# Gate logits of a graph network: narrow matrix products on TensorE, or row sums on VectorE in the later superblocks

## Chip, core and metric

The kernel runs on one core of a Trainium2 chip. The metric is device time in microseconds (us) of one execution, given as the median of several runs. A separate execution was taken with the hardware profiler; the lines shown in this document come from its page and its trace.

## What is computed

The reference is a graph network with 10000 nodes of 512 features and 160000 edges, in two layers. What matters here is the first layer, and of it one line:

```
gates = softmax(x @ gate_W + gate_b)          # gate_W is 512 x 4
top_v, top_i = top_k(gates, 2)                # two of four experts for each node
each expert: h = relu(mean_of_neighbours(h) @ Wl + bl + h @ Wr), twice
out = sum over the two chosen experts of top_v * expert output
```

The four numbers `x @ gate_W + gate_b` of a node are its gate logits. The second layer is an attention over the same edges, in which source and destination change their roles, so the edges have to be put in another order for it. The kernel does that sorting itself, during the first layer.

## The kernel before

**Tiling.** The nodes are cut into 79 blocks of 128, one node on each partition. Two blocks are a superblock (the first one has a single block), so there are 40 superblocks, numbered `s` = 0 to 39. The kernel runs in three stages. The first (the loop in lines 1227 to 1282) does the first convolution of all four experts, the gate logits, and the sorting. The second gathers the results for the second convolution and makes queries, keys and values. The third is the attention and what follows it. The change lies in the first stage.

**One superblock of the first stage**, in the order of the code: `drive(more, 1)` runs two of the ten gathering rounds of the next superblock; then come the gate logits of this one; then for each expert `e` the function `conv` (64 products for each `h`, line 1190, with a ScalarE activation into `h`, line 1192), two more gathering rounds, and from `e` = 1 on `products` of the expert before (line 1200, results stored to `y_tab` and `h_tab` in lines 1205 and 1206). At the end `turned_all` transposes the next superblock's rows into `tt` (line 1174), and the last `products` follows.

**Gathering.** A round takes the feature rows of four groups of edges out of a ring of ten buffers, multiplies them with one-hot matrices into `p_ag` (line 1151), and then issues with `pull` (line 1126) the indirect DMAs on GpSimd that fill the buffers used ten places later. `prepare` builds the one-hot matrices for a later block on VectorE (lines 902 and 1137). `load_x` brings the block's own 128 x 512 rows, `xb`, from two buffers; `turned_all` reads them.

**Gate logits.** For each block four products of the transposed rows in `tt` with the 128 x 4 pieces of `gw` go into a PSUM tile `pg` (line 1244), and VectorE adds `gb` to it on the way to `gate_w` (line 1246). In the trace each float32 product is two matrix instructions, so a block has eight and a superblock sixteen. At `s` = 12, 25, 38 and 39 the function `gates` turns the collected logits into the choice of experts.

**Sorting.** The generator `plan_src` counts, on VectorE, how many edges belong to each window of 32 nodes (158 counting steps, line 930) and then searches a slot for each edge. `side`, called after each quarter of a `conv`, advances it. When the search has ended, `side` puts a 1 into the list `planned`, and from then on it advances `scatter_src` instead: groups of 16 indirect DMAs (line 1060) from a tile `pay`, seven DMAs in each `conv`. The first of these starts at 1563.8 us in the trace, between the gate products of superblock 15 (which start at 1552.0 us) and those of superblock 16.

**Order.** In the first stage the order of the instructions on TensorE, VectorE, ScalarE and GpSimd is the order of the code (`manual_schedule`). The queue of SyncE, which issues the plain DMAs, is ordered by the compiler's scheduler. Each engine takes its instructions in that order and waits on semaphores. A pool tile with a `bufs` count is handed out again only after every reader of its former content is done.

Of the kernel before, what the change touches and what calls it, by code (L numbers as in the profile page):

```python
# [8 lines left out]
F32 = mybir.dt.float32  # L9
BF16 = mybir.dt.bfloat16  # L10
# [3 lines left out]
ALU = mybir.AluOpType  # L14
# [4 lines left out]
P = 128  # L19
D = 512  # L20
KD = D // P
NE = 4
# [595 lines left out]
WP = 2 + H  # L618
# [18 lines left out]
def fast(ctx: ExitStack, tc: tile.TileContext, a: dict, out: bass.AP, bad: bass.AP):  # L637
# [8 lines left out]
    nc = tc.nc  # L646
# [3 lines left out]
    NB = -(-N // P)  # L650
    NP = NB * P
    C = E // P
    NW = NB * NQ
# [7 lines left out]
    NPR = NW // 2  # L661
# [36 lines left out]
    def load_w(pool, name, ap, k, n, eng=None):  # L698
        return load_to(pool.tile([P, k, n], F32, name=name), ap, eng)
# [61 lines left out]
    gate_w = mp.tile([P, NB, NE], F32, name="gate_w")  # L761
# [20 lines left out]
    wp = p1.enter_context(tc.tile_pool(name="p1w", bufs=1))  # L782
# [28 lines left out]
    with tc.tile_pool(name="win", bufs=1) as one, tc.tile_pool(name="win2", bufs=2) as two, \  # L811
# [26 lines left out]
        for t in range(T):  # L838
# [8 lines left out]
                                    accum_out=more[:, t:t + 1])  # L847
            b = beg[:, t:t + 1]
            nc.vector.scalar_tensor_tensor(b, row[:, t:t + 1], float(C), more[:, t:t + 1],
                                           op0=ALU.mult, op1=ALU.add)  # L850
# [4 lines left out]
            for dst, flat in ((d_w, flat_d), (s_w, flat_s)):  # L855
# [8 lines left out]
                                           op0=ALU.is_gt, op1=ALU.add)  # L864
# [3 lines left out]
                                           op0=ALU.mult, op1=ALU.add)  # L868
            for c in range(CAP):
                for src, to in ((loc, loc_t[t]), (idx, idx_t[t])):  # L870
# [9 lines left out]
                                op0=ALU.not_equal)  # L880


    for e in range(NE):
        load_to(wl[e], a["L0_gnn_Wl"][e, 0])
        load_to(wr[e], a["L0_gnn_Wr"][e, 0], nc.scalar)
    gw = load_w(wp, "gw", a["L0_gnn_gate_W"], KD, NE)
    gb = wp.tile([P, NE], F32, name="gb")
    nc.sync.dma_start(gb, rows_bcast(a["L0_gnn_gate_b"], NE))
    bl = wp.tile([P, NE, KD], F32, name="bl")
# [18 lines left out]
    SC = max(C, 2 * D)  # L908
# [7 lines left out]
    def plan_src(pool, ps):  # L916
# [3 lines left out]
        pair = pool.tile([P, SC], BF16, name="pair")[:, :C]  # L920
# [7 lines left out]
        for b in range(NPR):  # L928
            m = pool.tile([P, C], BF16, name="m")
            v.scalar_tensor_tensor(m, pair, float(b), digit, op0=ALU.is_equal, op1=ALU.mult,  # L930
                                   accum_out=count[:, b:b + 1])
            yield
        num = pool.tile([P, NPR, 2], F32, name="num")
        even, odd = num[:, :, 0], num[:, :, 1]
        whole(v, odd, count, 1.0 / DIG, -0.4552)
        v.scalar_tensor_tensor(even, odd, -DIG, count, op0=ALU.mult, op1=ALU.add)
        upper = pool.tile([P, P], F32, name="upper")
        nc.gpsimd.iota(upper, pattern=[[1, P]], base=0, channel_multiplier=-1,
                       allow_small_or_imprecise_dtypes=True)
        v.tensor_scalar(upper, upper, 0.0, None, op0=ALU.is_gt)  # L940
        flat = num.rearrange("p b q -> p (b q)")
        total = ps.tile([P, 512], F32, name="mm")
        nc.tensor.matmul(total[:, :NW], ones, flat, start=True, stop=True)
        first = ps.tile([P, 512], F32, name="mm")
# [6 lines left out]
        v.tensor_reduce(top[:, 1:2], total[:, :NW], axis=AX.X, op=ALU.add)  # L951
        v.tensor_scalar(fail[:, 2:3], top[:, 1:2], float(E), None, op0=ALU.not_equal)
        v.tensor_scalar(flat, total[:, :NW], float(SC_W * P), 0.0, op0=ALU.subtract, op1=ALU.max)
        left = pool.tile([P, NB, 2], F32, name="left")
        half = left.rearrange("p b h -> p (b h)")
        v.tensor_add(half, even, odd)
        whole(v, left[:, :, 0], left[:, :, 0], 0.25, 0.375)
        v.scalar_tensor_tensor(left[:, :, 1], left[:, :, 0], 4.0, left[:, :, 1],
                               op0=ALU.mult, op1=ALU.add)
# [80 lines left out]
    GS = 16  # L1040

    def scatter_src(pool):
        src_r = a["src"].rearrange("(p c) -> p c", c=C)
        dst_r = a["dst"].rearrange("(p c) -> p c", c=C)
        att_r = a["edge_attr_8"].rearrange("(p c) h -> p c h", c=C)
        for c0 in range(0, C, GS):
            n = min(GS, C - c0)
            ends = pool.tile([P, 2, GS], I32, name="ends", bufs=2)
            nc.sync.dma_start(ends[:, 0, :n], src_r[:, c0:c0 + n])
            nc.sync.dma_start(ends[:, 1, :n], dst_r[:, c0:c0 + n])  # L1050
            att = pool.tile([P, GS, H], F32, name="att", bufs=2)
            nc.sync.dma_start(att[:, :n, :], att_r[:, c0:c0 + n, :])
            nc.vector.tensor_single_scalar(ends[:, 0, :n], ends[:, 0, :n], P - 1,
                                           op=ALU.bitwise_and)
            pay = pool.tile([P, GS, WP], F32, name="pay", bufs=3)
            nc.gpsimd.tensor_copy(pay.bitcast(I32)[:, :n, 0], ends[:, 1, :n])
            nc.gpsimd.tensor_copy(pay[:, :n, 1], ends[:, 0, :n])
            nc.gpsimd.tensor_copy(pay[:, :n, 2:], att[:, :n, :])
            for c in range(n):
                inst = nc.gpsimd.indirect_dma_start(  # L1060
                    out=sorted1[:],
                    out_offset=bass.IndirectOffsetOnAxis(ap=addr_i[:, c0 + c:c0 + c + 1], axis=0),
                    in_=pay[:, c, :], in_offset=None, bounds_check=P * NC - 1, oob_is_err=False)
                tc.declare_no_dep(inst.ins, group="sorted1", reason="rows of their own")
                tc.add_to_no_dep_group("sorted1", inst.ins)
                yield
# [47 lines left out]
    with p1, tc.tile_pool(name="p1k", bufs=1) as kp, tc.tile_pool(name="p1", bufs=2) as dp, \  # L1114
# [67 lines left out]
            return tt  # L1182

        def conv(tt, e, n):
            h = dp.tile([P, KD, 2 * P], F32, name="h", bufs=4)
            for f in range(KD):
                ph = pm.tile([P, D], F32, name="mm")
                for i, w in enumerate((wl[e], wr[e])):
                    for k in range(KD):
                        nc.tensor.matmul(ph[:, :n], w[:, k, f * P:(f + 1) * P], tt[:, i, k, :n],  # L1190
                                         start=(i + k == 0), stop=(i == 1 and k == KD - 1))
                nc.scalar.activation(h[:, f, :n], ph[:, :n], AF.Relu, bias=bl[:, e, f:f + 1])  # L1192
                side(e, f)
            return h
# [16 lines left out]
        planned, planning = [], [0]  # L1211
# [15 lines left out]
        with tc.manual_schedule(engines={ET.PE, ET.DVE, ET.Activation, ET.Pool}):  # L1227
            for i in range(GB):
                pull(i)
            prepare(0)  # L1230
            gated, GSTEP = 0, 13
            rows = []
            drive(gather(0, rows), CAP)
            tt = turned_all(rows)
            for s in range(NSB):
                n = P * len(rows)
                ahead = []
                more = gather(s + 1, ahead) if s + 1 < NSB else iter(())

                drive(more, 1)  # L1240
                for i, (b, xb, ag) in enumerate(rows):
                    pg = psm.tile([P, NE], F32, name="small")
                    for k in range(KD):
                        nc.tensor.matmul(pg, tt[:, 1, k, i * P:(i + 1) * P], gw[:, k, :],
                                         start=(k == 0), stop=(k == KD - 1))
                    nc.vector.tensor_add(gate_w[:, b, :], pg, gb)
                h = []
                for e in range(NE):
                    h.append(conv(tt, e, n))
                    if s == NSB - 1:  # L1250

                        load_to(wl[e], a["L0_gnn_Wr"][e, 1])
                        if e < 3:
                            nc.scalar.dma_start(wr[e], wqkv_s[e])
                    drive(more, 1)
                    if e == 0:

                        upto = SB[s][-1] + 1
                        if s == NSB - 1 or s % GSTEP == GSTEP - 1:
                            with tc.tile_pool(name="gates", bufs=1) as gt:  # L1260
                                gates(gt, gated, upto)
                            gated = upto
                    else:
                        products(s, h[e - 1], e - 1, n)
                rows = ahead
                if ahead:
                    tt = turned_all(ahead)
                products(s, h[3], 3, n)
                if s >= 1:
                    drive(fill, 11)  # L1270
                if s == max(NSB - 3, 0):
                    drive(plan, 10 ** 6)
                    drive(fill, 10 ** 6)
                    t3 = kp.tile([P, SC], F32, name="scan")[:3]
                    t1 = kp.tile([P, SC], BF16, name="pair")[:3]
                    for i, n in enumerate("qkv"):
                        nc.sync.dma_start(t3[:1, :D], a[f"L1_gnn_b{n}"][None, :])
                        nc.sync.dma_start(t3[:1, D:2 * D], fold_s[i:i + 1, :])
                        nc.vector.tensor_add(t3[:1, :D], t3[:1, :D], t3[:1, D:2 * D])
                        nc.sync.dma_start(bias_s[i:i + 1, :], t3[:1, :D])  # L1280
                    for i, n in enumerate(("bo", "b2")):
                        split_rows(t3[:, :D], t3[:, D:2 * D], t1[:, :D], i, a[f"L1_gnn_{n}"])


    with ExitStack() as p2:
        wp = p2.enter_context(tc.tile_pool(name="p2w", bufs=1))
# [8 lines left out]
        dp = p2.enter_context(tc.tile_pool(name="p2", bufs=2))  # L1295
# [72 lines left out]
        with tc.manual_schedule(engines={ET.PE, ET.Pool}):  # L1368
# [47 lines left out]
            for b in range(NB):  # L1416
                xb = load_x(dp, b)
# [29 lines left out]
                for v in range(2):  # L1447
                    nc.vector.scalar_tensor_tensor(t[v], p_ag[v], inv_deg[:, b:b + 1], t[v],
                                                   op0=ALU.mult, op1=ALU.add)
# [11 lines left out]
    with ExitStack() as p3:  # L1461
        wp = p3.enter_context(tc.tile_pool(name="p3w", bufs=1))
# [487 lines left out]
```

## Time and profile before

| | |
|---|---|
| median of 3 runs | 10796.1 us (10785.83 to 10797.64) |
| the profiled execution, its own time | 10026.75 us |
| span of the profiled execution, first to last instruction | 10025.0 us |
| mean granted TensorE clock in it | 0.981 |
| busy time of TensorE (matrix products) | 9375.0 us, 94% |
| busy time of VectorE | 5435.3 us, 54% |
| busy time of GpSimd | 6933.2 us, 69% |
| gate products (line 1244) | 632 instructions, from 100.5 to 3884.1 us |

The profiled execution is shorter than the runs that were timed. All durations below come from the profiled one. Busy time of an engine is a sum over the span and says nothing about which engine sets the time in a given stretch; for that one looks at a stretch of its own, and at which engine never waits there.

### The profile page before, as it was taken

How to read it: one execution, taken by the hardware profiler on the slowest of the kernel's cores; microseconds unless marked ns; L12 is line 12 of the kernel's file. 1: busy time of each engine (PE TensorE's matmuls, PEld its weight loads, DVE VectorE, ACT ScalarE, POOL GpSimd, SP SyncE). 2: the span in 40 equal slices, each digit the busy share in tenths (PEclk: the TensorE clock that was granted, in tenths of full speed). 3: DMA queues.
4: the chain of work that ended last, by engine and by line, in shares of the span. 5: the costliest groups of instructions: out<-in, count | busy, mean ns of one | idle time of the engine just before them, and what ended most of it. 6: DMA issues, size and time to landing. Idle time of an engine off the chain costs nothing.

```text
span 10025.0 us, 168607 instructions
## 1 busy us (share of the span) xinstructions
PE 9375.0 (94%) x63334; PEld 5488.9 (55%) x63334; DVE 5435.3 (54%) x8330; ACT 2927.5 (29%) x6026; POOL 6933.2 (69%) x6736
## 2 busy tenths in 40 slices
PE   7999999999999999999999999998888888888888
PEld 4666666666666666333333333333555555555555
DVE  7898991000100002445555555555888878888885
ACT  1111111111111111111111111111566666666665
POOL 5566666777777774777777777775666666666664
PEclk9999999999999999999999999998999999999999
DMA  6544455555555554888888888886878877777774
GB/s 213 179 154 155 158 162 162 155 159 156 163 168 156 164 157 160 281 297 298 299 294 300 297 303 302 297 299 215 255 254 257 256 252 252 254 256 255 252 253 132
DMA packets 1077231, 2263.27 MB, mean 226 GB/s; under 512 B 250526, under 2 KB 500260, under 8 KB 1075638
## 3 DMA queue, kind: packets, MB, share of 16 engines
q0 software_dynamic: 588224, 1659.68, 51.6%
q1 hardware_dynamic: 479456, 577.23, 16.6%
q10 hardware_dynamic: 8726, 15.49, 0.4%
q8 instruction: 503, 8.24, 0.3%
q14 instruction: 322, 2.64, 0.1%
HBM read 2181.26 MB, written 379.27 MB: 255 GB/s over the span
## 4 chain that ended last, share of the span: by engine, by line
PE 55%; DMA 16%; issue 9%; DVE 8%; ACT 7%; POOL 5%; POOLq 0%; ACTq 0%; DVEq 0%; SPq 0%
PE mm L1190 21%; PE mm L1200 10%; DMA kv<-kv_all,meta 7%; PE mm L1385 5%; DMA y<-y_tab,ix 5%; PE p_ag L1151 3%; DMA ring<-y_tab,ix 3%; PE p_ag L1426 3%; PE bank L1646 2%; DVE s L1879 2%; DVE m L930 2%; PE bank L1636 2%; PE mm L1347 2%; POOL y L1330 2%; ACT L1638 1%
## 5 line engine op out<-in xcount | busy, mean ns | idle before, releaser
L1126 POOL DMA_INDIRECT ring<-in_x_dram,idx_t x1580 | 1897.1, 1201 | 1014.3 <-PE p_ag L1151 570.3
L1190 PE MATMUL mm<-tt,big 128*128 128x256 f32 (+1 forms) x8960 | 1964.7, 378 | 0.0
L1190 PEld LDWEIGHTS mm<-tt,big 128*128 128x128 f32 x8960 | 1684.3, 191 | 285.3 <-issue 71.2
L1060 POOL DMA_INDIRECT sorted<-pay,addr x1250 | 1280.0, 1024 | 380.4 <-issue 336.8
L1552 POOL DMA_INDIRECT kv<-kv_all,meta x948 | 972.3, 1026 | 260.1 <-issue 144.5
L1330 POOL DMA_INDIRECT y<-y_tab,ix x920 | 947.5, 1030 | 287.8 <-issue 216.9
L1200 PE MATMUL mm<-wn,h 128*128 128x512 f32 x2528 | 1124.0, 598 | 0.0
L1385 PE MATMUL mm<-big,hb 128*128 128x512 f32 x2528 | 1120.4, 597 | 1.7 <-DMA hb<-h_tab 1.7
L1192 ACT ACTIVATE h<-mm,bl 128x256 f32<-128x256 f32 (+1 forms) x640 | 301.2, 471 | 2125.5 <-PE mm L1190 2125.5
L1714 POOL TENSOR_TENSOR ohp<-oh,p 128x768 f32<-128x768 bf16 x316 | 465.8, 1474 | 572.3 <-ACT p L1705 571.0
L1330 POOL DMA_INDIRECT ring<-y_tab,ix x660 | 684.7, 1037 | 228.6 <-issue 150.7
L1347 PE MATMUL mm<-big,z_t 128*128 128x512 f32 x1896 | 829.6, 594 | 0.7 <-ACT z_t L1340 0.7
L1385 PEld LDWEIGHTS mm<-big,hb 128*128 128x128 f32 x2528 | 469.7, 191 | 597.3 <-issue 532.8
L1388 DVE TENSOR_TENSOR mine<-mm,bias 128x512 f32<-128x512 f32 x316 | 218.5, 692 | 1065.2 <-PE mm L1385 1063.6
L1200 PEld LDWEIGHTS mm<-wn,h 128*128 128x128 f32 x2528 | 469.6, 191 | 594.0 <-issue 593.9
L1636 PE MATMUL bank<-big,big 128*128 128x256 f32 (+1 forms) x2560 | 671.7, 410 | 89.6 <-ACT big L1638 89.5
L1843 DVE TENSOR_TENSOR kv<-qe,kv 128x1024 f32<-128x1024 f32 x474 | 576.4, 1216 | 256.2 <-DMA kv<-kv_all,meta 255.1
L1426 PE MATMUL p_ag<-y,oh 128*32 128x512 f32 x3680 | 580.3, 600 | 77.4 <-DMA y<-y_tab,ix 77.1
L902 DVE TENSOR_TENSOR oh<-loc_t,iota_w 128x640 f32<-128x640 bf16 x158 | 131.3, 831 | 928.0 <-PE p_ag L1151 850.1
L1636 PEld LDWEIGHTS bank<-big,big 128*128 128x128 f32 x2560 | 501.2, 204 | 207.9 <-ACT big L1638 113.4
L1347 PEld LDWEIGHTS mm<-big,z_t 128*128 128x128 f32 x1896 | 362.0, 191 | 455.2 <-issue 429.8
L1646 PE MATMUL bank<-big,big 128*128 128x512 f32 x1264 | 592.4, 598 | 1.2 <-ACT big L1620 0.7
(298 smaller groups left out, 13882.7 us busy)
## 6 DMA issues: line engine op xcount, KB each, us to landing
y_tab<-y SPq DMA_DIRECT2D x632, 256.0 KB
hb<-h_tab SPq DMA_DIRECT2D x316, 256.0 KB
h_tab<-h SPq DMA_DIRECT2D x156, 512.0 KB
kv_all<-kvt SPq DMA_DIRECT2D x79, 520.0 KB
xb<-in_x_dram SPq DMA_DIRECT2D x156, 256.0 KB
q_all<-q SPq DMA_DIRECT2D x79, 384.0 KB
q<-q_all SPq DMA_DIRECT2D x237, 128.0 KB
ring<-in_x_dram,idx_t POOLq DMA_INDIRECT x1580
```

Source lines behind the costliest of these rows:

```text
L1060: inst = nc.gpsimd.indirect_dma_start(out=sorted1[:], out_offset=bass.IndirectOffsetOnAxis(ap=addr_i[:, c0 + c:c0 + c + 1], axis=0), in_=p ...
L1126: nc.gpsimd.indirect_dma_start(out=gbuf[i % GB], out_offset=None, in_=x, in_offset=bass.IndirectOffsetOnAxis(ap=window(idx_t, b)[:, j, c:c ...
L1190: nc.tensor.matmul(ph[:, :n], w[:, k, f * P:(f + 1) * P], tt[:, i, k, :n], start=(i + k == 0), stop=(i == 1 and k == KD - 1))
L1200: nc.tensor.matmul(py, h[:, k, i * P:(i + 1) * P], wn[e][:, k, :], start=(k == 0), stop=(k == KD - 1))
L1330: nc.gpsimd.indirect_dma_start(out=ybuf[i % YB], out_offset=None, in_=y_flat, in_offset=bass.IndirectOffsetOnAxis(ap=ahead[b][1][:, j, c:c ...
L1347: nc.tensor.matmul(po, z_t[:, k, :], wqkv[i][:, k, :], start=(k == 0), stop=(k == KD - 1))
L1385: nc.tensor.matmul(pr, hb[:, k, :], wr[e][:, k, :], start=(k == 0), stop=(k == KD - 1))
L1426: nc.tensor.matmul(p_ag[v][j * W:(j + 1) * W, :], oh[:, j * CAP + c, :], g[:, v * D:(v + 1) * D], start=(c == 0), stop=(c == CAP - 1))
L1552: nc.gpsimd.indirect_dma_start(out=to, out_offset=None, in_=kv_all[:], in_offset=bass.IndirectOffsetOnAxis(ap=blocks[b][0].bitcast(I32)[:, ...
L1636: nc.tensor.matmul(ph, up(f, k), z_t[:, k, :m], start=(k == 0), stop=(k == KD - 1))
L1646: nc.tensor.matmul(po, hid[:, k, i * P:(i + 1) * P], w2[k // KD][:, k % KD, :], start=(k == 0), stop=False)
L1843: nc.vector.tensor_tensor(k, qe.pop((w, g)).rearrange("p c (h d) -> p c h d", h=H), k, op=ALU.mult)
```

## The change

For each superblock that comes after the end of the slot search (`planned` is not empty), the gate logits are no longer made by TensorE. VectorE multiplies `xb` with a copy of `gate_W` that lies whole on every partition (`gate_rows`, 512 x 4 values), one column of the four at a time, and sums along the row in the same instruction (`accum_out`); the product itself goes to a tile that nobody reads. Then it adds `gb`. The superblocks ahead of the end of the search keep the products on TensorE.

One more DMA on SyncE's queue loads `gate_rows`. To make room for it, `h` gets three buffers and not four, `pay` gets two and not three, and `num`, `upper` and `left` of the search lie together in a tile that shares its place with the search's other scratch tile `scan`.

```
+    gate_rows = wp.tile([P, D, NE], F32, name="gate_rows")
+    gate_wt = a["L0_gnn_gate_W"]
+    nc.sync.dma_start(gate_rows, bass.AP(tensor=gate_wt.tensor, offset=gate_wt.offset,
+                                         ap=[[0, P], [1, D * NE]]))
     gb = wp.tile([P, NE], F32, name="gb")
...
-        num = pool.tile([P, NPR, 2], F32, name="num")
+        room = pool.tile([P, SC], F32, name="scan")
+        num = room[:, P:P + NW].rearrange("p (b q) -> p b q", q=2)
...
-        upper = pool.tile([P, P], F32, name="upper")
+        upper = room[:, :P]
         nc.gpsimd.iota(upper, pattern=[[1, P]], base=0, channel_multiplier=-1,
...
-        flat = num.rearrange("p b q -> p (b q)")
+        flat = room[:, P:P + NW]
...
-        left = pool.tile([P, NB, 2], F32, name="left")
-        half = left.rearrange("p b h -> p (b h)")
+        left = room[:, P + NW:P + NW + NPR].rearrange("p (b h) -> p b h", h=2)
+        half = room[:, P + NW:P + NW + NPR]
...
-            pay = pool.tile([P, GS, WP], F32, name="pay", bufs=3)
+            pay = pool.tile([P, GS, WP], F32, name="pay", bufs=2)
...
-            h = dp.tile([P, KD, 2 * P], F32, name="h", bufs=4)
+            h = dp.tile([P, KD, 2 * P], F32, name="h", bufs=3)
...
                 for i, (b, xb, ag) in enumerate(rows):
+                    if planned:
+
+                        unread = kp.tile([P, SC], BF16, name="pair")[:, :D]
+                        for e in range(NE):
+                            nc.vector.scalar_tensor_tensor(
+                                unread, xb, 1.0, gate_rows[:, :, e], op0=ALU.mult, op1=ALU.mult,
+                                accum_out=gate_w[:, b, e:e + 1])
+                        nc.vector.tensor_add(gate_w[:, b, :], gate_w[:, b, :], gb)
+                        continue
                     pg = psm.tile([P, NE], F32, name="small")
                     for k in range(KD):
                         nc.tensor.matmul(pg, tt[:, 1, k, i * P:(i + 1) * P], gw[:, k, :],
```

## Prediction, made before the changed kernel had run

> **What bounds the kernel now.** I read the slices first, saw that TensorE is full for most of the first stage, and then asked for busy time by stretches and for the waits of one quiet stretch. The stretches (length, busy time and instruction count of each engine, granted clock, DMA share, GB/s), one with the search of slots on VectorE and one behind it:
>
> ```profile
> 500.00:1000.00 500.00, 500.00 (x2248) 344.77 (x2244) 445.87 (x270) 79.38 (x153) 330.46 (x208) 1.00 0.49 155
> 2000.00:2500.00 500.00, 500.00 (x2236) 343.01 (x2235) 27.19 (x59) 80.07 (x154) 357.72 (x378) 1.00 0.51 159
> ```
>
> TensorE (first pair) has no idle time in either; VectorE (third) falls from 446 us to 27 us; GpSimd (fifth) is at 358. The waits between 2000 and 3500 us (total, times, longest) say who waits for whom:
>
> ```profile
> ACT h L1192 <- PE mm L1190: 813.1, 244, 6.7
> DVE oh L902 <- PE p_ag L1151: 577.6, 31, 22.4
> POOL ring L1126 <- PE p_ag L1151: 121.2, 28, 7.3
> PEld p_ag L1151 <- DMA ring<-in_x_dram,idx_t: 5.0, 15, 0.3
> ```
>
> Everybody waits for TensorE; it waits 0.3 us at most for a gathered row. So this stage lasts as long as TensorE's list of instructions. The chain of waits over one superblock (start, length, what) shows that list without a hole:
>
> ```profile
> 2036.13 1.85 PE p_ag L1151 x16
> 2037.98 1.88 PE small L1244 x16
> 2039.86 13.92 PE mm L1190 x64
> 2053.78 1.00 PE p_ag L1151 x8
> 2054.78 0.31 PE small L1159 x2
> 2055.09 0.99 PE p_ag L1151 x8
> 2056.08 14.01 PE mm L1190 x64
> 2070.09 1.85 PE p_ag L1151 x16
> ```
>
> The gate products (L1244) start again at 2135.17, so a superblock takes 97.19 us, and the gate is 1.88 us of it. The view of that line from 1564 us on counts what the change removes:
>
> ```profile
> L1244 PE MATMUL small<-gw,tt x384: 170/253/274, 1649.2 to 3884.1; 128*128 128x4 f32 x192
>   DVE gate_w L1246: 423.8, 48
> ```
>
> 384 instructions are 24 superblocks of 16, numbers 16 to 39; VectorE waited for them 48 times, once for each block.
>
> [...] 1.88 us over 16 is 118 ns each for 4 columns[...]. [...] The trace has 748 ns for such an instruction, and I use that. [...] pulls (L1126) have a median of 1327 ns from 600 to 1500 us, with VectorE busy, and 998 ns from 2000 to 3500 us. [...]
>
> **The change, part by part.**
>
> 1. *Gate products removed.* 24 superblocks. What follows the products changes its neighbour: conv's 64 products take 13.92 us behind the gate and 14.01 us where they follow p_ag directly (the row at 2056.08). So 1.88 + 13.92 - 14.01 = 1.79 us each, 24 x 1.79 = **43.0 us** off TensorE, all of it on the path. tt has been written by then: the transposes lie a whole set of products (6.87 us) ahead.
>
> 2. *Row sums on VectorE.* Eight for a superblock. Nearest row: the float32 scalar_tensor_tensor of L1394, and for the accumulator's read the 83 ns behind each L930:
>
> ```profile
> L1394 DVE SCALAR_TENSOR_TENSOR t<-mine,pick,t 128x512 f32<-128x512 f32 x474 | 335.1, 748 | 5.5
> L1137 DVE TENSOR_REDUCE slots<-oh 128x128 f32<-128x640 f32 x79 | 99.3, 1257 | 2.7
> L1320 DVE TENSOR_REDUCE at<-mp 128x20 f32<-128x640 f32 x79 | 64.2, 812 | 0.0
> ```
>
> The two reductions read equally many elements, L1137 with a wide step and L1320 in a row: a step can cost 1257/812 = 1.55. So one row sum is 0.83 us at the low end and 748 x 1.55 = 1.16, with the read 1.24 us, at the high end; eight with the two additions are 7.0 to 10.2 us. Cost on the path: **0**. They need only xb, loaded the superblock before, and follow one_hot and slots on VectorE, which end at 2119.9. So they end at 2126.9 to 2130.1. VectorE's next instruction, inv_deg, waits for the L1159 products at 2152: 22 us of cover remain. If VectorE were busy with the search, as up to 1500 us, there would be no such cover; the change leaves those superblocks alone.
>
> 3. *xb is held longer.* Its load for the next superblock now waits for the row sums too. SyncE issues both loads at 2126.28, right behind the transposes:
>
> ```profile
> 2126.28 1.42 SPq L715 DMA_DIRECT2D xb<-in_x_dram  x2
> 2130.57 5.27 SPq L1205 DMA_DIRECT2D y_tab<-y  x4
> ```
>
> Row 0 is done by 2123.2 to 2125.0, row 1 by 2126.9 to 2130.1, so at worst the second load slips 3.8 us and pushes the y_tab stores queued behind it on SP by about 1. ScalarE's y copies wait for those; TensorE has four PSUM tiles in hand. xb itself is needed 90 us later. Cost 0; up to 1 us a superblock (24) if that cover is gone.
>
> 4. *GpSimd.* Its list doesn't change, but a superblock gets 1.8 us shorter. It idles 121.2 us in 15.4 superblocks, 7.9 each, on p_ag; 6.1 remain. Tightest is the sixth pull behind the rounds at 2053.78: it ends at 2064.5 and is used near 2071.7, 7.2 us later. In the chain at the kernel's start such rows land in 2.5 to 4.8 us, so 2.4 to 4.7 are spare, and 0.6 to 2.9 after the change. Cost 0, but thin.
>
> 5. *gate_rows' load.* 1 MB on SP between gw and gb. Until about 75 us the DMA engines are 9 tenths busy and move about 390 GB/s: 1.05 MB are 2.7 us. Behind it wait bl and wn, and beside it the gathers for the first block; from 100 to 350 us the chain runs on through VectorE's counting, so a late start passes on. Bounds: 0 (the end is set by landing times with a pause in between) to 5.4[...]. I take **+2.7**.
>
> 6. *Fewer buffers, shared scratch.* h with three: the buffer that conv(e) writes was read by products(e-3), two convs and a store earlier, over 20 us. pay with two: 16 scatters stand between, some 55 us. The iota into the shared tile ends at 340.7, VectorE needs it at 354.9; should it now wait for VectorE, +0.5 once. Sum **0**, bounds 0 to 1. Stage two starts with other SBUF neighbours: -3 to +3, taken as 0.
>
> Sum: -43.0 + 2.7 = **-40.3 us**; against the profiled execution 10026.75 becomes 9986. The median of the runs, 10796.1, is 7.7% above that execution and nothing in the profile says why. I subtract the same microseconds: **10756**. If all of the 7.7% were a slower TensorE, the 43.0 would be 46.3.
>
> **Rivals.** (A) *The gain is partly lost to late rows.* Point 4's reserve fails in part, or SP's queue slips: 0.5 to 1.5 us a superblock, 12 to 36 us back, so -28 to -4: 10768 to 10792. For it: 0.6 us of reserve at the tight end. Against: the 0.3 us maximum wait now.
>
> (B) *GpSimd becomes the bound; slower.* If row sums lock GpSimd out for their whole time, it loses 6.6 to 9.9 us a superblock where it has 7.9 idle. From 7.9 on the superblock is longer than today; at 9.9 it is 2.0 longer, +48, with the load +51: 10847. Against: while L930, also with two SBUF inputs, ran without a pause, a pull took 1.20 us (331 to 339 us), not twice its 1.00. At that rate eight row sums cost GpSimd 2 us, under its 6.1.
>
> (C) *The switch doesn't come when I think*: `planned` set late, or the search slowed by its shared tile, by n superblocks: 1.8 us less each; five would leave -31, 10765. The search's code is otherwise the same, so this is small.
>
> **How the numbers follow.** Forecast 0.80 (10744 to 10765), A 0.11, B 0.06, C 0.03. About 0.2%, 21.6 us, is what a measurement of this kernel can tell from no change. Faster by more than that: forecast, C and a third of A, 0.86; within: most of the rest of A, 0.08; slower: B, 0.06. The range takes in A's better half, C, a gain scaled with the clock and some spread of the runs: 10740 to 10776.
>
> **What would show it.** Right: L1244 falls from 632 to 248 instructions; from superblock 16 on the period is 95.4 us and TensorE stays without idle time; row sums of 0.8 to 1.2 us on VectorE right behind slots; pulls still wait for p_ag. Wrong: TensorE waiting for gathered rows by more than 0.3 us each (A), pulls over 1.3 us behind 1650 us and no wait of GpSimd for p_ag (B), more than 248 left (C), or a first conv more than 6 us later.

## The result, and the profile after

| | median | lowest to highest | runs |
|---|---|---|---|
| before | 10790.97 us | 10774.18 to 10797.64 | 4 |
| after | 10858.1 us | 10836.35 to 10874.77 | 4 |

The ratio is 1.0063, with a 95% interval of 1.004 to 1.0086: the change makes the kernel slower by 67 us, where 40 us less were forecast. The profiled execution of after took 10836.35 us itself (span 10834.5 us, mean granted clock 0.959), so this profile, unlike that of before, is one of an execution like those that were timed.

First what was forecast to be seen. The view of the gate's line has the 248 instructions left (x, shortest/median/longest ns, first and last start):

```profile
L1258 PE MATMUL small<-gw,tt x248: 252/253/273, 100.7 to 1555.0; 128*128 128x4 f32 x124
```

The switch comes where it was expected. But the two stretches of the prediction (length, then busy time of TensorE, its weight loads, VectorE, ScalarE and GpSimd, granted clock, DMA share, GB/s) read so in the profile of after:

```profile
500.00:1000.00 500.00, 500.00 (x2246) 343.39 (x2239) 445.31 (x270) 79.52 (x153) 339.49 (x207) 1.00 0.49 155
2000.00:2500.00 500.00, 460.85 (x1909) 302.87 (x1909) 58.96 (x115) 68.23 (x134) 328.47 (x335) 0.95 0.44 139
```

The first is as before. In the second TensorE is idle for 39 us, runs 5% under its clock, and gets through 1909 matrix instructions where before had 2236 (some 82 of those, 16 in each 97.19 us, were the gate's). The waits of after between 2000 and 3500 us (total, times, longest) don't name anybody for it:

```profile
POOL ring L1131 <- PE p_ag L1156: 214.3, 32, 16.3
PEld mm L1195 <- issue: 209.4, 279, 2.5
PE mm L1195 <- issue: 110.1, 147, 2.2
```

"issue" is time in which an engine waited for nothing that the profile shows. GpSimd waits for TensorE more than before (214 us against 121), and the same view has TensorE waiting for gathered rows twice, 0.7 us in all, so GpSimd isn't what holds TensorE up. The timeline of TensorE in after shows what happens inside one `conv` (start, length, what, and in brackets the idle time ahead):

```profile
2058.10 7.11 PE L1205 MATMUL mm<-wn,h 128*128 128x512 f32 x16
2065.05 1.89 PE L1195 MATMUL mm<-tt,big 128*128 128x256 f32 x8
2067.05 0.59 PE L1195 MATMUL mm<-tt,wr 128*128 128x256 f32 x2
2069.16 0.38 PE L1195 MATMUL mm<-tt,wr 128*128 128x256 f32 x1 [1.52 <-issue]
2069.89 0.52 PE L1195 MATMUL mm<-tt,wr 128*128 128x256 f32 x1 [0.36 <-issue]
2071.26 0.59 PE L1195 MATMUL mm<-tt,wr 128*128 128x256 f32 x1 [0.85 <-issue]
2072.69 1.19 PE L1195 MATMUL mm<-tt,wr 128*128 128x256 f32 x2 [0.84 <-issue]
```

Products that follow each other every 0.22 us in an undisturbed `conv` (14.0 us over 64) come one at a time, with starts about 0.7 or 1.4 us apart (2069.16, 2069.89, 2071.26, 2072.69). I call these gaps **pauses**. The clock's records then show half speed from 2070.16 us on for 10.24 us. The profile of before that the prediction used has no pause in the first stage: behind the first scatter no two starts on TensorE in a row are over 0.6 us apart there.

Each group of runs has its own runs of the kernel before beside it, and there are groups in which TensorE pauses behind 1565 us (the kernel before takes 10769 to 10791 us) and groups in which it doesn't in the first stage (10025 to 10029 us): the times behind the prediction were of the first kind, the profile behind it of the second.

### The profile page after: what moved, and what is told of

Same layout as the page of the kernel before. It is cut to its first block, busy times and chain, and to the rows that moved or that the text cites. A ratio compares the mean times of both kernels' runs of the same rounds, so it can differ in the third digit from the quotient of the medians.

```text
span 10834.5 us, 168258 instructions
## 1 busy us (share of the span) xinstructions
PE 9739.4 (90%) x62950; PEld 5568.7 (51%) x62950; DVE 5526.8 (51%) x8714; ACT 2928.5 (27%) x6026; POOL 6962.6 (64%) x6736
## 5 line engine op out<-in xcount | busy, mean ns | idle before, releaser
L1131 POOL DMA_INDIRECT ring<-in_x_dram,idx_t x1580 | 1988.7, 1259 | 1287.3 <-PE p_ag L1156 754.7
L1195 PE MATMUL mm<-tt,big 128*128 128x256 f32 (+1 forms) x8960 | 2076.0, 386 | 148.2 <-issue 143.7
L1195 PEld LDWEIGHTS mm<-tt,big 128*128 128x128 f32 x8960 | 1712.9, 194 | 536.2 <-issue 310.3
L1065 POOL DMA_INDIRECT sorted<-pay,addr x1250 | 1263.9, 1011 | 380.4 <-issue 358.5
L1399 PE MATMUL mm<-big,hb 128*128 128x512 f32 x2528 | 1206.2, 619 | 120.8 <-issue 111.0
L1361 PE MATMUL mm<-big,z_t 128*128 128x512 f32 x1896 | 871.1, 612 | 114.1 <-DVE mine L1402 66.7
L1464 ACT ACTIVATE t<-t,gsel 128x512 f32<-128x512 f32 x158 | 109.2, 722 | 2138.9 <-DVE t L1462 1162.1
L1650 PE MATMUL bank<-big,big 128*128 128x256 f32 (+1 forms) x2560 | 629.8, 390 | 54.6 <-ACT big L1652 53.7
L1440 PE MATMUL p_ag<-y,oh 128*32 128x512 f32 x3680 | 608.9, 599 | 58.2 <-issue 43.4
L1440 PE MATMUL p_ag<-ring,oh 128*32 128x512 f32 x2640 | 562.6, 602 | 46.5 <-issue 29.8
```

The lines of the kernel that those rows point to most:

```text
L1065: inst = nc.gpsimd.indirect_dma_start(out=sorted1[:], out_offset=bass.IndirectOffsetOnAxis(ap=addr_i[:, c0 + c:c0 + c + 1], axis=0), in_=p ...
L1131: nc.gpsimd.indirect_dma_start(out=gbuf[i % GB], out_offset=None, in_=x, in_offset=bass.IndirectOffsetOnAxis(ap=window(idx_t, b)[:, j, c:c ...
L1361: nc.tensor.matmul(po, z_t[:, k, :], wqkv[i][:, k, :], start=(k == 0), stop=(k == KD - 1))
L1399: nc.tensor.matmul(pr, hb[:, k, :], wr[e][:, k, :], start=(k == 0), stop=(k == KD - 1))
L1440: nc.tensor.matmul(p_ag[v][j * W:(j + 1) * W, :], oh[:, j * CAP + c, :], g[:, v * D:(v + 1) * D], start=(c == 0), stop=(c == CAP - 1))
L1650: nc.tensor.matmul(ph, up(f, k), z_t[:, k, :m], start=(k == 0), stop=(k == KD - 1))
```

## The experiments

### The same kernels again, with profiles of the kind that was timed

The kernel before, unchanged, was run once more (e1), and the changed kernel too, with two variants: e3 keeps all else of the change (buffers, shared scratch, `gate_rows`) but leaves every gate product on TensorE, and e4 makes the later logits on neither engine.

```
e3:  -  if planned:
     +  if planned and False:
e4:  -  for e in range(NE):
     -      nc.vector.scalar_tensor_tensor(unread, xb, 1.0, gate_rows[:, :, e], ...)
     -  nc.vector.tensor_add(gate_w[:, b, :], gate_w[:, b, :], gb)
     +  nc.vector.tensor_copy(gate_w[:, b, :], gb)
```

> The unchanged kernel, profiled once more, because the profiled execution shown for it (10026.75 us) is 7.7% shorter than its timed runs and shows no pause of TensorE between single products, while the changed kernel's profile has many from about 1632 us on, in steps of 0.70 us and with no wait to explain them. Theory P (TensorE is paced from outside the program whenever it has been full for long, in both kernels): about 10790 us, with the same pauses of 0.70 and 1.40 us in the first and second stages, 700 us of them in all. Theory L (the new layout and buffers are to blame) and theory V (the row sums on VectorE are to blame): pauses absent from this kernel's first stage, superblocks of 97.19 us as in the first profile.

> The changed kernel as it is, beside the others on one chip. All theories: 1.004 to 1.009 of the kernel before. P: the row sums don't touch TensorE, its pauses take back the 43 us and more; L and V: as much slower as in its first measurement, with the loss inside the first stage behind superblock 16.

> The changed kernel with all its loads, buffers and shared tiles, but the gate logits on TensorE in every superblock, so that only the layout, the load of gate_rows and the buffer counts differ from the kernel before. L: the whole loss is here, 1.005 to 1.009. P and V: 0.999 to 1.001, plus 3 us for the load.

> The changed kernel without the row sums: for superblocks 16 to 39 the logits are left out and gate_w is filled with the bias, so neither TensorE nor VectorE does them. V: the 43 us are gained, 0.996. L: as slow as the changed kernel. P: no gain or a small one, since the pacing gives back what narrow products no longer take; between 0.998 and 1.006. The choice of experts differs from the reference, the amount of work doesn't.

| this against before (10769.22 us) | median | ratio | 95% |
|---|---|---|---|
| e1, unchanged | 10770.34 | 0.9997 | 0.9978 to 1.0015 |
| e2, the change | 10862.4 | 1.0079 | 1.0056 to 1.0102 |
| e3, the change without the switch | 10749.54 | 0.9992 | 0.9974 to 1.001 |
| e4, neither products nor row sums | 10868.01 | 1.0095 | 1.0079 to 1.011 |

The loss repeats. It isn't the layout, the buffers or the load (e3), and it isn't the row sums (e4 has none of them and is as slow). It comes with taking the products away.

The profile of e1 (10773.53 us) has pauses as well. Groups of TensorE from 1600 to 4200 us, in e1, then in e3, then in e2 (count | busy us, mean ns | idle us ahead of them and what ended it):

```profile
L1190 PE MATMUL mm<-tt,big 128*128 128x256 f32 x5248 | 1202.6, 385 | 48.3 <-issue 46.3
L1151 PE MATMUL p_ag<-ring,oh 128*32 128x512 f32 x1888 | 321.7, 620 | 43.4 <-issue 39.5
L1190 PE MATMUL mm<-tt,wr 128*128 128x256 f32 x768 | 208.0, 403 | 33.9 <-issue 32.4
```

```profile
L1195 PE MATMUL mm<-tt,big 128*128 128x256 f32 x5205 | 1224.1, 390 | 89.4 <-issue 85.9
L1156 PE MATMUL p_ag<-ring,oh 128*32 128x512 f32 x1856 | 300.6, 612 | 33.3 <-issue 30.7
L1195 PE MATMUL mm<-tt,wr 128*128 128x256 f32 x752 | 203.1, 404 | 31.4 <-issue 30.4
```

```profile
L1195 PE MATMUL mm<-tt,big 128*128 128x256 f32 x5175 | 1266.0, 396 | 150.9 <-issue 145.7
L1156 PE MATMUL p_ag<-ring,oh 128*32 128x512 f32 x1840 | 248.7, 604 | 7.0 <-issue 6.2
L1195 PE MATMUL mm<-tt,wr 128*128 128x256 f32 x736 | 209.9, 416 | 44.4 <-issue 42.4
```

In e1 a third of the idle time lies in the gathering products `p_ag`. In e2 it has left them and lies in the products of `conv`: 195 us against 82. e3, which keeps the gate products as e1 does, has 33 us in `p_ag` and 121 in `conv`. The same stretches as a whole, e1 first, then e2:

```profile
1600.00:4200.00 2600.00, 2461.83 (x10298) 1606.03 (x10290) 160.50 (x420) 365.19 (x715) 1638.36 (x1725) 0.97 0.45 140
```

```profile
1600.00:4200.00 2600.00, 2387.26 (x9683) 1536.76 (x9682) 358.16 (x783) 353.81 (x692) 1665.25 (x1695) 0.94 0.44 137
```

75 us less of TensorE's busy time, and the clock down from 0.97 to 0.94. From the traces I worked out how long each kernel takes between the first scatter (near 1565 us) and the end of the first stage, with the sum of the clock's records at half speed in it, and the length of the second stage:

| profile | first scatter to end of stage one, us | of it at half clock | stage two |
|---|---|---|---|
| before, the prediction's profile (no pauses) | 2403.4 | 0 | 2967.4 |
| e9, the change (no pauses) | 2361.1 | 0 | 2962.2 |
| e1, before | 2708.3 | 184 | 3356.6 |
| e3, layout only | 2754.0 | 232 | 3364.0 |
| after | 2780.4 | 328 | 3365.5 |
| e2, the change | 2784.0 | 321 | 3378.1 |
| e4, neither | 2804.9 | 352 | 3369.3 |

Each row is a single execution. Without pauses the change shortens the rest of stage one by 42 us, as forecast. With them it is 72 to 76 us longer than in e1, but only 26 to 30 longer than in e3; and e3, whose profiled execution (10807.41 us) lies 58 us above its median, is itself 46 us above e1, though the two differ only in layout, buffers and the load. So in these traces pauses and half clock cost some 70 to 120 us more with the change (42 us more than those differences). The medians of whole executions are firmer: the change loses 67.1 and 93.2 us where TensorE pauses (10858.1 - 10790.97 and 10862.4 - 10769.22) and gains 43.7 where it doesn't (e9, below), so what it forfeits to pauses is 111 to 137 us. The half clock alone explains some 50 to 70 us of stage one, if time at half clock loses half its length (328 less 232 or 184, halved; an estimate). Stage two differs by 22 us at most among the five profiles with pauses.

### Is it the narrowness, the time, or the row sums?

The next question was what the gate products had done for the kernel: a rest for TensorE because they are narrow, or merely 1.8 us of work in that place. Five edits:

```
e5   (before)  +  if planned:           # per block, ahead of the gate products
               +      relief(KD)        # four more products of 4 columns
e6   (after)   +  relief(KD)            # behind the row sums: both of them
e7   (after)   row sums out;  +  filler(2)   # two products of 256 columns per block
e8   (before)  +  if planned and e:     # ahead of conv 1 to 3
               +      relief(KD)
e9             the changed kernel as it is
```

> The kernel before, with as many narrow products again (4 columns, into a PSUM tile that nobody reads) ahead of the gate products in superblocks 16 to 39: 43 us more on TensorE's list. Theory P (narrow products are a rest from a pacing of TensorE, and without them the pauses grow): faster than the kernel before, down to 0.991 if the second group is worth as much as the first, 0.998 to 1.000 if one group already rests it enough. Theory S (the list's length decides, and the loss of the changed kernel has another cause): 1.004.

> The changed kernel with its row sums on VectorE, and with as many narrow products as before kept on TensorE at the old place (their result is not read). P: 0.998 to 1.002, the row sums cost nothing and the loss was the missing products. Theory V (the row sums cost time of themselves): 1.006 to 1.010.

> As the run without any gate behind the plan (logits left out for superblocks 16 to 39), but with products of 256 columns at the gate's place, 4 for a superblock, some 1.75 us, of the same kind as conv's, result not read. If it is the narrowness of the products that rests TensorE: 1.010 to 1.014, since 42 us of full work come on top of the run without gates. If it is only the time or the place between p_ag and conv: 0.999 to 1.002, as the kernel before.

> The kernel before, with four more narrow products (0.9 us, result not read) ahead of the second, third and fourth conv of superblocks 16 to 39: 65 us more on TensorE's list. P: the pauses lie in those convs, so a rest ahead of each takes most of them away: 0.980 to 0.992. S: 1.006.

These were measured in a group without pauses, which can't answer that question, and neither could the next two groups, but for what they say of the list of TensorE itself. e10, e11 and e12 repeat e6, e7 and e8 beside e9, the changed kernel; e13, e14 and e15 repeat them once more.

> The changed kernel once more, beside the kernels of the last group, because that group ran where the kernel before takes 10029 us and its TensorE never pauses, and the first two measurements of the change where it takes 10770 to 10790 us and pauses. Theory P: where the kernel before pauses, 1.006 to 1.009 again; where it doesn't, 0.996, since 43 us of narrow products go from a list without pauses. Theory V (row sums cost time): slower in both.

> Row sums on VectorE, and the narrow products kept on TensorE, result not read. Where TensorE doesn't pause this was 0.9993. Where it pauses, P: 0.998 to 1.002; V: 1.006 to 1.010.

> No gate behind the plan (logits left out for superblocks 16 to 39), four products of 256 columns in its place, result not read. Where TensorE doesn't pause this was 0.9998. Where it pauses: 1.010 to 1.014 if the narrowness is what rests it, 0.999 to 1.002 if it is the time or the place.

> Four more narrow products ahead of the second, third and fourth conv of superblocks 16 to 39, 65 us more on the list. Where TensorE doesn't pause this was 1.006. Where it pauses, P: 0.980 to 0.992, most of the pauses gone; S (length of the list): 1.006.

> Row sums on VectorE, and the narrow products kept on TensorE, result not read; 1.0002 where TensorE doesn't pause. Where it pauses, P (the missing products are the cause): 0.998 to 1.002; V (the row sums cost time): 1.006 to 1.010.

> Four wide products in the gate's place, result not read, logits left out for superblocks 16 to 39; 0.9993 where TensorE doesn't pause. Where it pauses: 1.010 to 1.014 if narrowness is the rest, 0.999 to 1.002 if it is the time or the place.

> Narrow products ahead of three more convs, 65 us more on the list; 1.006 where TensorE doesn't pause. Where it pauses, P: 0.980 to 0.992; if the pauses don't heed such a rest: 1.004 to 1.010.

| no pauses; before is 10025 to 10029 us | ratio (95%) |
|---|---|
| **e9, the change** | 0.9953 (0.9939 to 0.9967), 9982.86 us |
| row sums and products: e6, e10, e13 | 0.9993 (0.9984 to 1.0001), 1.0002 (0.9994 to 1.0011), 0.9998 (0.9989 to 1.0006) |
| 256 columns in the gate's place: e7, e11, e14 | 0.9998 (0.999 to 1.0007), 0.9993 (0.9986 to 1.0), 1.0001 (0.9993 to 1.0009) |
| narrow products ahead of each conv: e8, e12, e15 | 1.006 (1.0047 to 1.0074), 1.0062 (1.0048 to 1.0075), 1.007 (1.0057 to 1.0084) |
| e5, the gate's products twice | 1.0114 (1.0099 to 1.013), 10145.35 us |

e5 lies outside what either theory forecast for it; the last section returns to it. In these groups the change gains 43.7 us (10026.57 - 9982.86), and e6, e10 and e13 show that VectorE's row sums cost nothing: with the products put back the time of before is back. The lines of e9 that answer to the prediction: the stretch from 2000 us, the waits between 2000 and 3500 us, and the row sums from 1600 to 3900 us:

```profile
2000.00:2500.00 500.00, 500.00 (x2202) 338.75 (x2201) 80.84 (x155) 83.67 (x161) 377.44 (x386) 1.00 0.53 161
```

```profile
DVE inv_deg L1167 <- PE small L1164: 664.8, 31, 21.7
POOL ring L1131 <- PE p_ag L1156: 52.6, 21, 3.4
PEld p_ag L1156 <- DMA ring<-in_x_dram,idx_t: 0.6, 2, 0.4
```

```profile
L1251 DVE SCALAR_TENSOR_TENSOR pair<-xb,gate_rows 128x512 bf16<-128x512 f32 x192 | 212.9, 1109 | 7.8 <-DMA rows_s<-pair 2.8
L1251 DVE DVE_READ_ACCUMULATOR pair<-xb,gate_rows 128x1 f32 x192 | 17.2, 89 | 0.0
```

TensorE has no idle time, its waits for gathered rows are 0.4 us at most, and behind the row sums VectorE still waits 21.7 us for TensorE.

### Back where TensorE pauses

e16 is the kernel of e7, and e17 that of e8, in a group with pauses (before 10780.84 us).

> Wide products in the gate's place, result not read, logits left out for superblocks 16 to 39; 0.9993 to 1.0001 where TensorE doesn't pause. Where it pauses: 1.010 to 1.014 if narrowness is the rest, 0.999 to 1.002 if it is the time or the place.

> Narrow products ahead of three more convs, 65 us more on the list; 1.006 to 1.007 where TensorE doesn't pause. Where it pauses, P: 0.980 to 0.992; if the pauses don't heed such a rest: 1.004 to 1.010.

e16 took 10803.33 us, 1.0012 (0.9996 to 1.0028); e17 took 10855.92 us, 1.0067 (1.0045 to 1.009). The groups of TensorE from 1600 to 4200 us in e16, then in e17, then in e4 for comparison:

```profile
L1195 PE MATMUL mm<-tt,big 128*128 128x256 f32 x5425 | 1213.4, 381 | 24.6 <-issue 23.9
L1156 PE MATMUL p_ag<-ring,oh 128*32 128x512 f32 x1872 | 337.4, 616 | 56.9 <-issue 49.7 <-DMA sorted<-pay,addr 0.8
```

```profile
L1190 PE MATMUL mm<-tt,big 128*128 128x256 f32 x5248 | 1198.0, 384 | 37.7 <-issue 35.9
L1151 PE MATMUL p_ag<-ring,oh 128*32 128x512 f32 x1872 | 345.4, 606 | 54.9 <-issue 48.2 <-DMA sorted<-pay,addr 0.4
```

```profile
L1195 PE MATMUL mm<-tt,big 128*128 128x256 f32 x5150 | 1271.1, 398 | 154.8 <-issue 149.4
L1156 PE MATMUL p_ag<-ring,oh 128*32 128x512 f32 x1824 | 245.0, 604 | 6.4 <-issue 5.5
```

The kernels of e16 and e4 differ in one thing: four products of 256 columns per superblock, 8 instructions of 0.22 us or 1.7 us in all, where the gate had been. With them there are 57 us of idle time in `p_ag` and 25 in the group of `conv` shown; without, it is the other way round (6 and 155). e4 is 0.9% slower than the before of its group, and e16 as fast as the before of its own within its interval. So the products needn't be narrow: a theory that narrow products give TensorE a rest falls with e16, and is not helped by e17, where three more groups of them don't take the pauses away and cost 0.7%, as much as without pauses (0.6 to 0.7%). In all the profiles with pauses the idle time of `p_ag` from 1600 to 4200 us is 33 to 57 us where some 1.7 to 1.9 us of TensorE work stand in the gate's place (e1, e3, e16, e17), and 6 to 7 us where none does (after, e2, e4). Why such work moves the pauses isn't shown, nor that it has to stand in this place: no run left the gate's place empty and put the work elsewhere.

Three limits of this reading. Neither e4 nor the change was run in the group of e16, so ratios of two groups are compared. In e16 the rest of stage one took 2661.6 us, 47 less than in e1, with 68 us at half clock; but stage two, in which nothing differs, took 3459.1 us, 102 more, so pauses differ between stages and groups too, and the profiled execution of e16 (10831.88 us) is 28 us above its median. And the mixture of row sums and products (e6) was never run in a group with pauses.

### What makes TensorE pause?

In all the profiles with pauses, none comes in the steady superblocks before the first scatter (TensorE is busy for the whole 500 us from 500 to 1000 us), and the first comes 22 to 67 us behind it. I counted as a pause a start on TensorE that comes over 0.5 us later behind the one before it than is usual for the two lines. In the rest of stage one the traces then have 0.13 to 0.21 pauses per us while GpSimd issues scatters (L1065, L1060 in before), and 0.004 to 0.07 while it issues pulls. That is an association. The scatters alone aren't enough: before and e9 issue the same 694 of them in stage one, without a single pause there. e18 was to test the association: the changed kernel with the scatters left for stage two.

```
e18:     if planned:
     -       drive(scat, 2 if f < KD - 1 else 1)
     +       return
```

> The changed kernel with every scatter of the sorting left to the second stage and its end; the total is some 900 us longer for that (697 scatters at 1.3 us behind the second stage), and only the first stage is looked at. Theory D (pauses of TensorE follow the scatter DMAs): no pauses between 1565 us and the end of the first stage, superblocks of 95.4 us, the stage's end near 3925 us, also where the kernel before pauses. Theory T (pauses come after TensorE has been full for some 1.6 ms): pauses from about 1630 us on as before, the end near 4350 us. Where the kernel before doesn't pause, it can't tell them apart: 3925 us in both.

It was measured in a group without pauses: 10872.81 us against 10025.42, 1.0847 (1.0829 to 1.0866). It shows what the scatters cost when they aren't hidden beside stage one, and nothing about the pauses. **Inconclusive.**

## Why the prediction was wrong, and where it was right

**The step that failed** is the sentence "this stage lasts as long as TensorE's list of instructions", and its use in the last sum. It was read from an execution in which TensorE has no hole, and it holds there (e9). The prediction saw that the median was 7.7% above that execution, said that nothing in the profile says why, and subtracted the same microseconds all the same; its only other reading was a slower TensorE, which would have scaled the 43.0 to 46.3. In e1, a profile of the kind that was timed, 694 us of the extra 747 of span (10771.7 - 10025.0) lie in the rest of stage one and in stage two, where the trace shows pauses and half clock. Then the stage is the list plus the pauses, and the pauses change with what is on the list. The prediction put that term at nothing. Taking 1.79 us away per superblock took 42 us out of the list and, by the medians, cost 111 to 137 us in pauses and half clock; by what mechanism stays open. No rival had this. B gave "slower" a chance of 0.06, for another reason: A and B looked for a late row or a locked GpSimd, and the waits of after and of e9 show neither (from 2000 to 3500 us TensorE waits twice for gathered rows in each, 0.7 and 0.6 us in all, and GpSimd still waits 214.3 and 52.6 us for `p_ag`).

**Point 1, gate products.** Right as a term. The superblocks behind the search take 97.19 us in before and 95.42 in e9, on average of 23 of them in the trace: 1.77 us each, where 1.79 were expected.

**Point 2, row sums.** Right. 1109 + 89 = 1.20 us each, inside 0.83 to 1.24, near the end with the step. The cover of 22 us was 21.7. The instruction, which reads a column of `gate_rows` with a step of four values, took 1109 ns in e9 against 748 for the contiguous one (L1394 in before), 1.48 times as long. But the two also differ in the sum along the row and in the bf16 output, so how much of that the step causes isn't shown, and that the factor came near the assumed 1.55 may be luck.

**Points 3 and 6, buffers.** Right that they cost nothing that can be measured: e3 is at 0.9992 (0.9974 to 1.001), and e6, e10 and e13 carry the same buffers.

**Point 4, GpSimd.** The sign was right, the size not. GpSimd's wait for `p_ag` fell from 121.2 to 52.6 us; that leaves 3.3 us a superblock, not 6.1. The groups of GpSimd from 2000 to 3500 us, before and then e9, show the missing part:

```profile
L1126 POOL DMA_INDIRECT ring<-in_x_dram,idx_t x620 | 623.5, 1006 | 301.8 <-issue 150.7 <-PE p_ag L1151 121.2 <-PE mm L1200 8.2
```

```profile
L1131 POOL DMA_INDIRECT ring<-in_x_dram,idx_t x627 | 672.9, 1073 | 237.4 <-issue 160.1 <-PE p_ag L1156 52.6 <-PE mm L1195 12.5
```

A pull is 67 ns longer on average; with 40 pulls in a superblock that is 2.7 us beside the row sums, where rival B was dismissed with 2. Rival B would have needed over 6, so it stays wrong.

**Point 5, the load of `gate_rows`.** Mis-sized, as far as single executions tell: 2.7 us were taken, and the first gate product starts at 100.7 us in after and 99.1 in e9, against 100.5 in before, so no such delay is seen. The time alone could not have told: e9's interval is a gain of 33 to 61 us, which holds both -40.3 and -43.0.

**Why pauses in `p_ag` should cost less is not shown.** At the place of after shown above, pauses in `conv` are followed by 10.24 us at half clock, and the kernels whose pauses lie in `conv` spend more time so (321 to 352 us of stage one in after, e2 and e4, 184 and 232 in e1 and e3, 68 and 58 in e16 and e17). That fits, but no run took the one away and left the other.

## What to carry to other kernels

When the profiled execution differs from the timed median by more than the effect that is forecast, it isn't yet a profile of what is timed: get one that matches before a term of it is subtracted, or put the unexplained part into the range with both signs. Here work taken off an engine that never waits was worth its time where nothing else stopped the engine (43.7 us gained), and not where something did (67.1 and 93.2 us lost); whether work that looks like pure cost also keeps such stops away has to be measured. The choice depends on the conditions here: the changed kernel is better by 0.5% where TensorE doesn't pause and worse by 0.6 to 0.8% where it does, and no version that was tried beat both kernels in both.

## What the runs showed of the hardware that was not expected

**Pauses without a named cause.** The same program takes some 10027 or 10770 us, depending on the group of runs; in the long executions TensorE pauses in steps of about 0.7 us (in the rest of stage one of after 101 starts come 0.70 to 0.75 us behind the one before, and 54 come 1.40 to 1.45 us behind it) and spends more time at half clock (in the rest of stage one 184 us in e1, none in the profile behind the prediction). Two groups on chips with the same number (e13 to e15, and e16 and e17) showed one kind each; whether it was the same chip isn't known, nor what sets the kind.

**Half clock without a long idle time.** In e5 the gate's products are doubled to 32 instructions of 4 columns. 24 superblocks of 1.8 us would be 43 us; it cost 116 (10145.35 - 10029.15). The timeline of TensorE in e5 shows one place:

```profile
2060.72 1.05 PE L1230 MATMUL small<-gw,tt 128*128 128x4 f32 x8
2061.63 1.03 PE L1251 MATMUL small<-gw,tt 128*128 128x4 f32 x8
2062.53 1.08 PE L1230 MATMUL small<-gw,tt 128*128 128x4 f32 x8
2063.75 1.84 PE L1251 MATMUL small<-gw,tt 128*128 128x4 f32 x8
2065.45 16.40 PE L1190 MATMUL mm<-tt,big 128*128 128x256 f32 x64
```

The last eight take twice as long, and the `conv` behind them 16.4 us where 14.0 are usual. The clock's records have half speed from 2063.38 us for 6.83 us, and then again each 102.40 us (2165.78, 2268.18, ...). 24 spells of 6.83 us, at half their length, are 82 us (an estimate), and with the 43 somewhat more than the 116. The spells come in steps: 116 of the 117 in after last a multiple of 3.41 us (56 of them 3.41, 23 6.83, 14 10.24, 6 20.48), as the 6.83 here does. No long idle time stands ahead of those looked at. In e5 the chain of waits from 2000 us to the place shown has 0.14 us of it, and half speed begins 2.7 us behind the first narrow product. In after no idle time of TensorE in the 15 us ahead of a spell, in the 29 spells of the rest of stage one, is longer than 1.72 us; at the place shown it is 1.52. What starts a spell isn't shown. Sixteen narrow instructions in the gate's place (before), with or without eight more ahead of each further `conv` (e8, the kernel of e12), come without such a loss: the granted clock from 1600 to 4200 us is 1.00 in both, where e5 has 0.97.
